# Three modulation vectors of an adaLN block: weights moving instead of stationary, with a transpose behind

## The chip, the cores and the metric

The kernel runs on one core of a Trainium2 chip. The metric is the device time of one execution in microseconds (us). Engines are named as the profile names them: PE is TensorE (PEld its weight loads), DVE is VectorE, ACT is ScalarE, POOL is GpSimd, and SP is the queue that issues most DMAs.

## The reference, cut to what matters

Two sub-blocks, a Mamba-like state-space layer and a stream-mixing layer, each stand behind a layer norm whose result is scaled and shifted by vectors made from a small conditioning input `c` (4 x 1024). A third vector gates each sub-block's output.

```python
mod = (_silu(L0_c) @ L0_wmod).reshape(4, 6, 1, -1)      # wmod is 1024 x 6144
sa, ca, ga, sb, cb, gb = (mod[:, i] for i in range(6))
ga = (2 * (ga >= 0) - 1) * jnp.maximum(jnp.abs(ga), 0.25)
gb = ...                                                # the same
h = _layernorm(x) * (1 + ca) + sa                       # x is 4 x 512 x 1024
x = x + ga * mamba(h, ...)                              # in_proj, conv, scan over time, out_proj
h = _layernorm(x) * (1 + cb) + sb
x = x + gb * mix_streams(h, ...)
```

All of it is fp32. This case is about `sa`, `ca` and `ga`.

## The kernel before

The work is split into 8 blocks (`NBLK`) of 256 time steps (`TB`), two to a batch row. A block of the scan has 64 steps: 4 groups of 512 channels by 16 state elements. One scan step has a product on POOL (`w`, L917), exponentials on ACT (`da`, L933), four scans on DVE (L963), eight transposes on PE (`hq`, L943) and two weighted sums on DVE (`acc`, L952).

Around the steps lie the matrix products: `pp` (L439) and `pz` (L487) are the in-projection, `po` (L667) the out-projection, `pd` (L597) the time-step projection. They are written as Python generators in one queue. Before the scan, the queue is run to its end (`whole()`), and the tile framework's scheduler sets the order of the instructions. In the scan the order is written out by hand: each step has six ticks, each tick lets the queue emit as many matmul columns as a rate allows (`paced`), and work that other code put on PE meanwhile is announced in columns with `aside` and taken off that rate. What follows a product, `finish()`, is spawned as a task that waits some ticks (`LAG` and others) before it emits. `take` and `give` count PSUM banks (`mm`, four) and SBUF rows (`row`, five); a waiting task tries again on a later tick.

Every product's weights come in tiles of 1 MB through three buffers (tag `wts`), loaded by SP (L218). `wmod` is cut in 24 such tiles: six kinds (`SA, CA, GA, SB, CB, GB`) by four quarters of 256 output columns.

There are two ways in which a kind is computed:

- `SA`, `CA` and `GA` (`product_mod`, L262): the weights are stationary, 128 x 128 at a time, and the 4 columns of `silu(c)` (`sc`) move through. The result comes out as 128 channels by 4 batch rows, all quarters in one PSUM bank, and one ACT instruction (L275 or L277) writes it to `mod_t`.
- `SB`, `CB` and `GB` (`product_rows`, L296): the 4 columns of `sc` are stationary and 256 columns of weights move. The result is 4 rows of 256, copied by ACT (L304) and stored to DRAM.

`SA` and `CA` are the first products of the kernel. `norm(0)` has loaded and normalized two tiles of `x` by then; it transposes them (L400) and scales and shifts them with `mod_t` (L409) into `ht`, on which `pp` of block 0 waits. After `whole()` the constants are loaded (`load_constants`). `GA` stands at the head of the queue in the scan of block 0, and `SB`, `CB`, `GB` come later in that block. `GA` is used first in block 1 (`product_out`).

Of the kernel before, what the change touches and what calls it, by code (L numbers as in the profile page):

```python
# [9 lines left out]
F32 = mybir.dt.float32  # L10
AF = mybir.ActivationFunctionType
# [5 lines left out]
P = 128  # L17
B, T, H = 4, 512, 1024
DIN, N, R, KC = 2048, 16, 64, 4
TB = 256  # L20
# [3 lines left out]
HC = H // P  # L24
# [8 lines left out]
LAG, TAP_LAG, ACT_LAG, POOL_LAG, DMA_LAG = 2, 3, 5, 10, 12  # L33
MAKE_UP = 1.3
TURN = 64
# [16 lines left out]
def adaln_block(  # L52
# [22 lines left out]
    vec, act, pool, pe = nc.vector, nc.scalar, nc.gpsimd, nc.tensor  # L75
# [7 lines left out]
    ident = const.tile([P, P], F32, name="ident")  # L83
# [17 lines left out]
    with ExitStack() as ph:  # L101
        p1 = ph.enter_context(tc.tile_pool(name="p1", bufs=1))
# [12 lines left out]
        done = set()  # L115
# [4 lines left out]
        def route(g):  # L120
            got = next(g, None)
            if got == "v":
                gaps.append(g)
            elif got is not None:
                waiting.append((clock[0] + max(got, 1), g))

        def spawn(g):
            route(g)

        def take(what, idle=1):  # L130
            while not free[what]:
                yield idle
            free[what] -= 1

        def give(what):
            free[what] += 1

        def until(key, idle=1):
            while key not in done:
                yield idle  # L140
# [58 lines left out]
        def aside(columns):  # L199

            owed[0] += columns
# [31 lines left out]
        def bank(name, shape):  # L233
            return ps_mm.tile(list(shape), F32, name=name, tag="mm")
# [4 lines left out]
        sc = p1.tile([P, HC, B], F32, name="sc")  # L239
# [5 lines left out]
        def away_from_zero(m, sg, ab):  # L245
            vec.tensor_scalar(sg, m, 0.0, 2.0, ALU.is_ge, ALU.mult)
            vec.tensor_scalar(ab, m, -1.0, 0.25, ALU.mult, ALU.max)
            vec.tensor_tensor(ab, ab, m, ALU.max)
            vec.scalar_tensor_tensor(m, sg, -1.0, ab, ALU.add, ALU.mult)

        pms = {}

        def product_mod(kind, q):

            if q == 0:
                yield from take("mm", 0)
                pms[kind] = bank(f"pm_{kind}", (P, HC, B))
            pm = pms[kind]
            w = weights.pop(("mod", kind, q))
            for j in range(2):  # L260
                for k in range(HC):
                    pe.matmul(  # L262
                        pm[:, 2 * q + j, :],
                        w[:, k, j * P : (j + 1) * P],
                        sc[:, k, :],
                        start=(k == 0),
                        stop=(k == HC - 1),
                    )
                    yield 128
            m = mod_t[:, kind]  # L270

            def finish():
                yield LAG
                if kind == CA:
                    act.activation(m, pm, AF.Copy, bias=1.0)  # L275
                else:
                    act.copy(m, pm)  # L277
                give("mm")
                if kind == GA:
                    yield ACT_LAG  # L280
                    yield "v"
                    sg = p1.tile([P, HC, B], F32, name="sg_ga", tag="ss")
                    ab = p1.tile([P, HC, B], F32, name="ab_ga", tag="sq")
                    away_from_zero(m, sg, ab)
                done.add(("mod", kind))

            if q == 3:
                spawn(finish())

        def product_rows(kind, q):  # L290

# [711 lines left out]
        with tc.manual_schedule():  # L1003
# [5 lines left out]
            for k in range(NBLK):  # L1009
# [9 lines left out]
                for s in range(STEPS):  # L1019
                    g = k * STEPS + s  # L1020
                    q, n = divmod(s, N)
# [15 lines left out]
    with ExitStack() as ph:  # L1037
        p1 = ph.enter_context(tc.tile_pool(name="f1", bufs=1))
# [29 lines left out]
        for i in range(NTT):  # L1068
            k, r = divmod(i, TT)
# [218 lines left out]
```

## Time and profile before

| what | value |
|---|---|
| three timed runs | 2709.05, 2709.85, 2709.86 us; median 2709.85 |
| the profiled execution | 2702.3 us, span 2700.5 us, mean granted TensorE clock 0.94 |
| L262, 128 x 4 | 384 records: 256 for SA and CA, 128 for GA |
| SA and CA on PE | first record at 9.06 us, `mod_t` complete at 66.50 us |
| first `pp` (L439) | 67.60 us |
| first scan step's transposes | 166.6 us |
| last GA record | 206.9 us |
| L296, 4 x 256 | 192 records, 271.4 to 331.4 us |

The profiled execution is one run, and its span is counted from the first to the last instruction. A row of the timeline gives start, duration, engine, line, operation, output and inputs with the count of merged instructions, and in brackets the idle time ahead of it and what ended that. A row of the windows gives, for a stretch of time, the busy time of each engine with its number of instructions, the granted clock, the busy share of the DMA engines and their GB/s. A busy TensorE is not one at its peak: the time of one record in a row of equal ones is better read from their spacing.

### The profile page before, as it was taken

What the parts mean: (1) busy time and instruction counts of PE and PEld (TensorE: products, weight loads), DVE (VectorE), ACT (ScalarE), POOL (GpSimd) and SP (SyncE); (2) the same over time, 40 slices, a digit from 0 to 9 for tenths busy, and PEclk for the clock granted to TensorE, in tenths of its full rate; (3) what the DMA queues carried; (4) which work ended last, traced back from release to release, by engine and by line L of the source; (5) the groups of instructions that cost most, each with busy time, mean ns of one, the idle gap of its engine ahead of it and who ended that gap; (6) DMA issues with size and microseconds to landing.
All of it is one profiled execution on the core that took longest, in us unless ns stands there. A gap on an engine that the chain in (4) does not pass through costs nothing. (4 is left out here: it accounts for less than half of the span.)

```text
span 2700.5 us, 39703 instructions
## 1 busy us (share of the span) xinstructions
PE 2408.1 (89%) x13392; PEld 2051.6 (76%) x13392; DVE 2361.0 (87%) x4451; ACT 1716.9 (64%) x3755; POOL 1731.8 (64%) x1167
## 2 busy tenths in 40 slices
PE   8999989999999989998999899998999899885446
PEld 8887478888788878887888788887888777675435
DVE  0349898999999999999999999999999899977898
ACT  0356567666776777667776776668666856633445
POOL 0146557777976688768766786779676977931014
PEclk9979989999999999999999999999999899896769
DMA  5432523333433343234333433333333323225302
GB/s 184 152 125 94 204 75 130 113 106 121 154 117 104 116 153 121 106 114 149 125 110 114 156 118 109 118 145 125 121 106 124 130 94 117 83 74 203 153 31 110
DMA packets 74347, 331.06 MB, mean 123 GB/s; under 512 B 8496, under 2 KB 25312, under 8 KB 47456
## 3 DMA queue, kind: packets, MB, share of 16 engines
q1 hardware_dynamic: 62784, 311.56, 32.1%
q10 hardware_dynamic: 11360, 16.96, 1.7%
q8 instruction: 107, 1.75, 0.3%
q14 instruction: 96, 0.79, 0.1%
HBM read 303.14 MB, written 25.35 MB: 122 GB/s over the span
## 5 line engine op out<-in xcount | busy, mean ns | idle before, releaser
L917 POOL TENSOR_TENSOR w<-u,b 128x1024 f32<-128x1024 f32 x512 | 1209.1, 2363 | 558.2 <-PE hq L943 413.5
L933 ACT ACTIVATE da<-dv,aneg 128x256 f32<-128x256 f32 x2048 | 971.5, 477 | 616.5 <-DVE w L963 571.5
L963 DVE TENSOR_TENSOR_SCAN w<-da,w 128x256 f32<-128x256 f32 x2048 | 1263.3, 667 | 69.5 <-ACT da L933 47.6
L952 DVE SCALAR_TENSOR_TENSOR acc<-hq,ss,acc 128x512 f32<-128x512 f32 x1024 | 724.6, 735 | 78.2 <-PE hq L943 73.1
L943 PE MATMUL hq<-ident,w 128*128 128x128 f32 x4096 | 644.1, 282 | 73.1 <-DVE acc L952 53.7
L943 PEld LDWEIGHTS hq<-ident,w 128*128 128x128 f32 x4096 | 511.8, 146 | 220.7 <-issue 57.7
L487 PE MATMUL pz<-w_z,ht 128*128 128x256 f32 x2048 | 517.2, 387 | 0.0
L439 PE MATMUL pp<-ht,w_x 128*128 128x259 f32 x2048 | 511.5, 387 | 0.0
L667 PE MATMUL po<-y,w_out 128*128 128x256 f32 x2048 | 496.2, 381 | 5.4 <-ACT dv L608 5.4
L439 PEld LDWEIGHTS pp<-ht,w_x 128*128 128x128 f32 x2048 | 372.1, 193 | 46.2 <-issue 0.4
L667 PEld LDWEIGHTS po<-y,w_out 128*128 128x128 f32 x2048 | 368.6, 191 | 46.5 <-ACT dv L608 6.9
L487 PEld LDWEIGHTS pz<-w_z,ht 128*128 128x128 f32 x2048 | 369.2, 195 | 36.5 <-issue 0.3
L455 DVE SCALAR_TENSOR_TENSOR xc<-pp,cw,xc 128x256 f32<-128x256 f32 x384 | 178.4, 464 | 31.8 <-ACT xc L448 30.7
L1212 POOL TENSOR_TENSOR o<-o,x 128x1024 f32<-128x1024 f32 x16 | 37.7, 2354 | 189.1 <-ACT dg L1158 142.2
L1197 PE MATMUL oa<-h,dg 128*128 128x256 f32 x256 | 62.8, 389 | 74.9 <-ACT dg L1158 69.5
L1197 PEld LDWEIGHTS oa<-h,dg 128*128 128x128 f32 x256 | 49.3, 195 | 84.1 <-ACT dg L1158 76.5
L467 POOL TENSOR_TENSOR xc<-xc,sx 128x1024 f32<-128x1024 f32 x32 | 75.5, 2358 | 42.8 <-ACT sx L465 42.8
L448 ACT ACTIVATE xc<-pp,cb,cw 128x256 f32<-128x256 f32 x128 | 71.3, 557 | 47.5 <-PE pp L439 47.4
L749 PE MATMUL py<-ident,acc 128*128 128x128 f32 x256 | 48.4, 324 | 54.7 <-ACT dv L608 28.3
L262 PEld LDWEIGHTS pm<-sc,w_mod 128*128 128x128 f32 x384 | 80.9, 323 | 9.0 <-DVE mv_a L358 9.0
L262 PE MATMUL pm<-sc,w_mod 128*128 128x4 f32 x384 | 79.5, 343 | 9.1 <-DMA w_mod<-wmod_dram 9.1
L749 PEld LDWEIGHTS py<-ident,acc 128*128 128x128 f32 x256 | 34.8, 167 | 67.2 <-ACT dv L608 25.2
(172 smaller groups left out, 2303.2 us busy)
## 6 DMA issues: line engine op xcount, KB each, us to landing
w_x<-in_w_dram SPq DMA_DIRECT2D x64, 1024.0 KB, 4.7
w_z<-in_w_dram SPq DMA_DIRECT2D x64, 1024.0 KB, 4.9
w_out<-out_w_dram SPq DMA_DIRECT2D x56, 1024.0 KB, 4.8
w_mod<-wmod_dram SPq DMA_DIRECT2D x24, 1024.0 KB, 4.8
b<-bcd SPq DMA_DIRECT2D x32, 512.0 KB, 3.8
xt<-x_dram SPq DMA_DIRECT2D x16, 512.0 KB, 8.2
xr<-x_dram SPq DMA_DIRECT2D x32, 256.0 KB, 5.1
x<-xr ACTq DMA_DIRECT2D x32, 256.0 KB, 2.5
```

The lines of the kernel that those rows point to most:

```text
L262: pe.matmul(pm[:, 2 * q + j, :], w[:, k, j * P : (j + 1) * P], sc[:, k, :], start=(k == 0), stop=(k == HC - 1),)
L439: pe.matmul(pp, w[:, h, j * P : (j + 1) * P], hts[k][:, h, :], start=(h == 0), stop=(h == HC - 1),)
L455: vec.scalar_tensor_tensor(xc[:, c, :], pp[:, tap : tap + TB], cw[:, i, tap : tap + 1], xc[:, c, :], ALU.mult, ALU.add,)
L487: pe.matmul(pz[:, t, :], hts[k][:, h, PAD + t * P : PAD + (t + 1) * P], w[:, h, :], start=(h == 0), stop=(h == HC - 1),)
L667: pe.matmul(po, w[:, d - lo, :], ys[k, d // QC][:, d % QC, :], start=(d == lo), stop=(d == hi - 1),)
L749: pe.transpose(py[:, j, t * P : (t + 1) * P], acc[:, t, c * P : (c + 1) * P], ident)
L917: pool.tensor_tensor(w, us[k, q], bts[k, n // NG][:, n % NG, :].unsqueeze(1).to_broadcast([P, QC, TB]), ALU.mult,)
L933: act.activation(da[:, j, :], dts[k, q][:, 2 * s + j, :], AF.Exp, scale=aneg[:, i, n : n + 1])
L943: pe.transpose(h[:, c * P : (c + 1) * P], ws[g][:, c, t * P : (t + 1) * P], ident)
L952: vec.scalar_tensor_tensor(acc[:, t, :], hqs.pop((g, t)), cts[k][:, t, n : n + 1], acc[:, t, :], ALU.mult, ALU.add,)
L963: vec.tensor_tensor_scan(w[:, c, :], das[g, c // 2][:, c % 2, :], w[:, c, :], 0.0, ALU.mult, ALU.add)
L1197: pe.matmul(oa[:, n, :], dg[:, n, m, :], hs[m] if m < NS else ybs[i], start=(m == 0), stop=(m == NS),)
```

## The change

`product_mod` now computes each quarter as `product_rows` does: `sc` is stationary, 256 weight columns move, and the result is 4 rows by 256 in a PSUM bank of its own. ACT copies each quarter into a row tile `mr` (4 x 1024). When the fourth quarter is there, eight transposes on PE bring the row into 128 channels by 4 batch rows (`pmt`), and ACT writes that to `mod_t` as before. The eight transposes are announced with `aside`. Nothing else is edited. Lines behind the edit move by 8: L439 becomes L447, L943 becomes L951.

```diff
-        pms = {}
+        mrows = {}
 
         def product_mod(kind, q):
 
-            if q == 0:
-                yield from take("mm", 0)
-                pms[kind] = bank(f"pm_{kind}", (P, HC, B))
-            pm = pms[kind]
+            yield from take("mm", 0)
             w = weights.pop(("mod", kind, q))
-            for j in range(2):
-                for k in range(HC):
-                    pe.matmul(
-                        pm[:, 2 * q + j, :],
-                        w[:, k, j * P : (j + 1) * P],
-                        sc[:, k, :],
-                        start=(k == 0),
-                        stop=(k == HC - 1),
-                    )
-                    yield 128
+            pm = bank(f"pm_{kind}_{q}", (B, TB))
+            for k in range(HC):
+                pe.matmul(pm, sc[:, k, :], w[:, k, :], start=(k == 0), stop=(k == HC - 1))
+                yield TB
             m = mod_t[:, kind]
 
             def finish():
                 yield LAG
+                if q == 0:
+                    yield from take("row")
+                    mrows[kind] = p1.tile([B, H], F32, name=f"mr_{kind}", tag="row", bufs=5)
+                    done.add(("mrow", kind))
+                yield from until(("mrow", kind))
+                mr = mrows[kind]
+                act.copy(mr[:, q * TB : (q + 1) * TB], pm)
+                give("mm")
+                if q < 3:
+                    return
+                yield LAG
+                yield from take("mm")
+                pt = bank(f"pmt_{kind}", (P, HC, B))
+                for i in range(HC):
+                    pe.transpose(pt[:, i, :], mr[:, i * P : (i + 1) * P], ident[:B, :B])
+                aside(HC * TURN // 2)
+                give("row")
+                yield LAG
                 if kind == CA:
-                    act.activation(m, pm, AF.Copy, bias=1.0)
+                    act.activation(m, pt, AF.Copy, bias=1.0)
                 else:
-                    act.copy(m, pm)
+                    act.copy(m, pt)
                 give("mm")
...
-            if q == 3:
-                spawn(finish())
+            spawn(finish())
```

## The prediction

> **What bounds the kernel now.** I read the page's busy shares first, then windows by stage, then TensorE's timeline where a stage is not like the others. Matmuls in fp32 leave two records each, transposes one; counts below are records.
>
> ```profile
> span 2700.5 us, 39703 instructions
> PE 2408.1 (89%) x13392; PEld 2051.6 (76%) x13392; DVE 2361.0 (87%) x4451; ACT 1716.9 (64%) x3755; POOL 1731.8 (64%) x1167
> ```
>
> The average names no bound: PE and DVE are level. By stage they part (columns: span, busy time and count of PE, PEld, DVE, ACT, POOL, granted TensorE clock, DMA share, GB/s):
>
> ```profile
> 9.03:43.00 33.97, 33.94 (x160) 33.97 (x161) 0.00 (x0) 2.56 (x3) 0.64 (x3) 1.00 0.46 172
> 184.06:191.53 7.47, 7.47 (x38) 7.47 (x37) 3.84 (x6) 3.55 (x9) 2.35 (x1) 0.50 0.36 132
> 280.00:324.52 44.52, 44.52 (x224) 18.97 (x223) 38.60 (x60) 21.13 (x56) 23.52 (x10) 1.00 0.59 206
> 860.00:1145.00 285.00, 270.26 (x1554) 233.15 (x1553) 268.14 (x462) 203.00 (x442) 215.06 (x143) 0.98 0.35 125
> ```
>
> The last line is the steady scan, where DVE has 17 us idle in 285. The first two are the stages of the edited product: PE has no idle time, DVE 0 or half. The third is the product of rows (L296), whose form the change copies. TensorE's timeline (start, duration, engine, line, operation):
>
> ```profile
> 9.06 34.26 PE L262 MATMUL pm<-sc,w_mod 128*128 128x4 f32 x160 [9.06 <-DMA w_mod<-wmod_dram]
> 43.19 2.80 PE L400 MATMUL pt<-ident,xt 128*128 128x128 f32 x12
> 45.78 20.48 PE L262 MATMUL pm<-sc,w_mod 128*128 128x4 f32 x96
> 66.55 1.11 PE L400 MATMUL pt<-ident,xt 128*128 128x128 f32 x4 [0.29 <-ACT mod_t L275]
> 67.60 58.94 PE L439 MATMUL pp<-ht,w_x 128*128 128x259 f32 x256
> ```
> ```profile
> 164.75 2.04 PE L400 MATMUL pt<-ident,xt 128*128 128x128 f32 x16
> 169.69 3.15 PE L262 MATMUL pm<-sc,w_mod 128*128 128x4 f32 x24
> 184.06 5.12 PE L262 MATMUL pm<-sc,w_mod 128*128 128x4 f32 x24
> 280.00 2.75 PE L296 MATMUL pmr<-w_mod,sc 128*4 128x256 f32 x12
> ```
>
> One L262 record costs 34.26/160 = 0.214 us at the start, 5.12/24 = 0.213 where the granted clock is 0.50, and 3.15/24 = 0.131 just before that. So the opening runs at half clock too, although its window prints 1.00 (transposes agree: 2.80/12 = 0.233 there, 2.04/16 = 0.128 at 164.75). One L296 record at full clock costs 0.2155 (2.75 us less the last one's 0.379, over 11).
>
> In the GA stage the waits of 166 to 208 say who is late:
>
> ```profile
> DVE acc L952 <- PE hq L943: 24.1, 11, 7.9
> ```
>
> DVE sits 24.1 us behind transposes that queue behind L262.
>
> **The change, part by part.** SA and CA at the start: 256 records go, 128 come.
>
> 1. Products. Removed: 256 x 0.214 = 54.7 us, all on the path. Added: 128 x 0.2155 = 27.6 us at full clock. Gain 27.1.
> 2. Clock. The first records still run at half. After L439 begins at 207.07 the granted clock is 0.83 from 208 to 212 and 1.00 after, so it came free some 2.5 us in; after the dt matmuls at 145.04 it took about 6 us. At half speed that loses 1.2 to 3 us. Taken: 2.5.
>
> Here a rule of the Trainium skill needs weighing (TensorE: Matmul & The Clock Gate, Part 1: The HAM clock gate): the clock is released after about 3.4 us of sustained matmuls. By the rule alone the opening would have been released by 13 us; the trace shows 57 us of unbroken L262 at the half-clock price, so being busy was not enough there. Whether the new product is enough is therefore read from L296: with the same 4-column weights and 256 moving columns the clock stays 1.00 for 44 us. The transposes around it do not explain that, as they are as many per step in the GA stage, at 0.50. By the rule or by L296 the sum is the 2.5 us above; by the L262 row (never released) 128 records cost 55 us and step 1 gains nothing. I take L296.
>
> 3. Tail, new on the path. As built, PE runs 8 transposes for SA, 6 for CA, three of the 16 x transposes, the last two for CA, then the other 13. A 4x128 to 128x4 transpose has no row; bounds are nothing and the half-clock L943 record (1.09/4 = 0.27); nearest is L262's own 128x4 record, so 0.131. From the last product to mod_t: 16 x 0.131 + 3 x 0.128 = 2.5 us on PE, which covers the last row copy (0.37 us by L304), then about 0.5 for the move into mod_t, then two L409 activations (1.07) before L439 begins: 4.1 us. Before, the same way was 66.26 (45.78 + 20.48) to 67.60, 1.3 us, and 12 x transposes (2.8) lay inside the products. Net: +2.8 for the longer tail, -2.8 for the transposes no longer there: 0.
>
> So L439 begins near 9.06 + 27.6 + 2.5 + 4.1 = 43.3, not 67.60: 24.3 us.
>
> 4. L439 itself. It starts at half clock now: 58.94 us against 128 x 2 x 0.2155 x 259/256 = 55.8 plus a last end, about 2.9 lost. A rule speaks against keeping this (same page, Part 4: PE-mode transpose: transposes do not count as busy for the clock); by it the 4 us tail of transposes cools the clock and the 2.9 stay lost. The row: 16 transposes at 164.75 and 8 after them run at 0.13 and the clock falls only at 172, over 5 us after the last wide product. I take the row, 2.9; the rule's zero goes into the range.
>
> 5. Loads. Hidden today by slow products, now closer. Each w_mod load is 1 MB and lands 4.8 us after issue; at 4 to 12 us the queue moves over 420 GB/s, 2.5 us per MB. A quarter now lasts 16 x 0.2155 = 3.45 us; its buffer's successor is wanted two quarters later, 6.9, against 4.8: 2.1 us slack. As built, five of the seven constant loads (0.6 MB, 0.4 to 0.6 us of SP each) stand between the w_mod loads instead of behind; dtw's half MB takes 1.3 of the slack. Zero taken; if the cover is gone, 2 to 4 us. The activation of aneg now stands before CA's last row copy on ACT; its load is issued after the last w_mod, three quarters (10 us) ahead: no wait. The row tiles of SA and CA make the second xt of block 1 wait on the first block's x transposes; on SP the ffn constants and the fourth w_x stand behind it, needed over 20 us later: zero.
>
> GA, in the scan. Removed: 128 records; added 64, 4 row copies, 8 transposes. DVE's scan groups begin at 172.24, 179.64, 184.97, 192.44, 200.33, 207.69, 213.10, then follow every 3.9 us or so. Up to 174.66 DVE is busy and nothing changes. The third group no longer waits behind slow dt matmuls and L262: about 177.6. The fourth then waits for ACT's two table loads and dv (until 180.06) and its da: 181.4. From there the mix is that of 280.00 to 324.52, ten steps in 44.52, 4.45 a step, PE-bound: 185.9, 190.3, 194.8, 199.2 against 213.10, 13.9 us. Eight transposes (1 us) and wide products landing in a step as before: 13. Bounds: 18 if steps fall to 4 us, 8 if the clock dips at the dt stage as it does at 332 to 342. The copies (368 ns by L304) lie on an ACT with half its time free; PSUM banks are now taken per quarter, as L296 does without starving PE.
>
> Later blocks. The three new notes of 256 aside columns hold the products back by 768/308 = 2.5 ticks, 0.4 of a step; as built the whole queue stands that much later in blocks 1 to 6, a b load goes ahead of a row load and that ahead of a w_z load on SP. DVE is the bound there and its instructions are the same. From 17 us idle per block I allow 2 either way in six blocks, 12, and take 0.
>
> Sum: 24.3 + 2.9 + 13 = 40 us. The profiled execution took 2702.3 (span 2700.5), so 2662; the three timed runs stand 7.5 us above it, and I expect that gap again: 2709.85 - 40 = 2670.
>
> **Rivals.** *Clock stays at half.* If four weight columns do not count as activity, and L296's clock was due to its company, a record costs twice 0.2155 = 0.43: 192 x 0.43 = 82.7 against 384 x 0.214 = 82.1, and 24 transposes at 0.27, late copies and the L439 start add 8: 2718, slower. It decides once the clock is at half for over three quarters of both stages. Against it: L296 at 1.00. For it: L262, busy and never released. 5%. *Start cold, GA full* (other products warm it there): the start loses about 5, GA keeps 13: 2702. 5%. *Loads bind*: if every load took the 8.8 us of the first (L218's longest), three buffers would turn over in 8.8 + 3.45, 4.1 us a quarter for 3.45, 3 us over five quarters; with 4 for the constants, 2677; inside the range, 10%. *Drift of the later blocks eats it*: 2 to 4 us in each of six blocks: 2682 to 2694; 8%, half inside. *The change misses the path*: not possible at the start, since nothing else runs there.
>
> **How the numbers follow.** The forecast 68%, loads 10%, drift 8% (half of it inside), a cold start 5%, a cold clock throughout 5%, better than 2656 by a drift the other way 4%. The range holds the first two and half of the third, 82%: 2656 is start 29, GA 18, drift +7; 2692 is start 20, GA 8, drift -10. Over 0.2% faster (5.4 us, about what a measurement of this kernel can tell): forecast, loads, better, most of drift and some of the cold start, 0.91; within 0.2%: the rest of those two, 0.04; slower: 0.05.
>
> **What would show it.** L259 records spaced 0.2155 from about 13 us on and 0.43 before; L439 beginning at 42 to 46; no w_mod wait on PE after the first; scan steps of 4.4 us in place of 7.4, hq waits of DVE before 200 us down from 24 to under 8; blocks of 285 us unchanged. Wrong: spacing near 0.43 past 20 us, holes on PE before a w_mod landing, or blocks of 288 and more.

## The result, and the profile after

The changed kernel takes 2703.43 us (median; 2699.0 to 2708.07) against 2709.98 us (2704.88 to 2717.91) for the kernel before, twelve runs each: the ratio is 0.9973, 95% interval 0.9964 to 0.9983. It is 6.5 us faster where 40 were forecast, and it lies outside the range of 2656 to 2692.

The first part of the working came out. TensorE's timeline of the changed kernel (start, duration, engine, line):

```profile
9.23 29.38 PE L259 MATMUL pm<-w_mod,sc 128*4 128x256 f32 x128 [9.23 <-DMA w_mod<-wmod_dram]
38.53 1.02 PE L279 MATMUL pmt<-ident,mr 4*128 4x4 f32 x14
39.49 0.55 PE L408 MATMUL pt<-ident,xt 128*128 128x128 f32 x3
39.97 0.28 PE L279 MATMUL pmt<-ident,mr 4*128 4x4 f32 x2
40.18 1.64 PE L408 MATMUL pt<-ident,xt 128*128 128x128 f32 x13
41.68 56.37 PE L447 MATMUL pp<-ht,w_x 128*128 128x259 f32 x256
```

All of SA and CA is one row of 128 records with a single wait ahead of it, the first load. `pp` begins at 41.68 us, was 67.60, and takes 56.37 us, was 58.94.

The steps of GA, in the same view later on:

```profile
151.66 2.75 PE L259 MATMUL pm<-w_mod,sc 128*4 128x256 f32 x12
156.04 2.75 PE L259 MATMUL pm<-w_mod,sc 128*4 128x256 f32 x12
169.70 0.65 PE L279 MATMUL pmt<-ident,mr 4*128 4x4 f32 x8
```

From 151.66 to 156.04 is one step of 4.4 us, the scan groups from 149.35 to 170.48 are 4.2 us apart on average, and GA is over at 170.35 (169.70 + 0.65). DVE's wait for transposes between 126 and 215 us, in the view of waits (total, times, longest), is 9.3 us, where 24.1 stood before (166 to 208 us); under 8 was forecast:

```profile
DVE acc L960 <- PE hq L951: 9.3, 4, 8.3
```

The longest wait in each sum does not belong to GA. It ends before the first GA record, which stands at 168.6 us before the change and at 142.6 after. DVE's timeline, before and after:

```profile
167.27 1.41 DVE L952 SCALAR_TENSOR_TENSOR acc<-hq,ss,acc 128x512 f32<-128x512 f32 x2 [7.85 <-PE hq L943]
140.54 1.41 DVE L960 SCALAR_TENSOR_TENSOR acc<-hq,ss,acc 128x512 f32<-128x512 f32 x2 [8.31 <-PE hq L951]
```

Without it, DVE waited 16.2 us in the GA stage before and 1.0 after.

So far the gain is there. Comparing when the same scan group begins in the two traces shows where it went (the first scan of each group of four on DVE, L963 before and L971 after):

| scan group | before, us | after, us | after less before (unrounded times) |
|---|---|---|---|
| block 0, step 0 | 154.6 | 127.4 | -27.2 |
| block 0, step 12 | 227.5 | 184.4 | -43.2 |
| block 1, step 0 | 470.4 | 432.1 | -38.3 |
| block 2, step 0 | 747.6 | 717.1 | -30.6 |
| block 3, step 0 | 1026.4 | 1004.1 | -22.3 |
| block 4, step 0 | 1306.9 | 1290.5 | -16.4 |
| block 5, step 0 | 1586.1 | 1577.5 | -8.6 |
| block 6, step 0 | 1867.3 | 1864.0 | -3.3 |
| block 7, step 0 | 2143.4 | 2148.4 | +5.1 |

The changed kernel was 43 us ahead at step 12 of block 0. Then each of blocks 1 to 6 took 5 to 8 us longer than before, and in the two profiled executions, of 2702.3 and 2703.51 us, all of the gain was given back; by the medians 6.5 us of it are left. The averages hardly tell: the page's busy shares, and the window of the prediction's steady scan (span, then busy time and count of PE, PEld, DVE, ACT, POOL, granted clock, DMA share, GB/s):

```profile
span 2701.6 us, 39388 instructions
PE 2384.0 (88%) x13224; PEld 1997.2 (74%) x13224; DVE 2362.9 (87%) x4451; ACT 1722.6 (64%) x3767; POOL 1732.1 (64%) x1167
```
```profile
860.00:1145.00 285.00, 265.46 (x1513) 229.17 (x1512) 261.58 (x451) 197.22 (x424) 212.29 (x147) 0.96 0.34 120
```

DVE, the bound of this stage, was busy 268.14 us in this window before and is now 261.58: 6.6 us of new idle time in about one block. The waits between 430 and 2150 us say what it waits for. Before:

```profile
DVE acc L952 <- PE hq L943: 23.7, 28, 2.0
PE hq L943 <- DVE acc L952: 18.3, 26, 2.6
PEld px L520 <- POOL xc L467: 2.2, 6, 0.5
PE px L520 <- POOL xc L467: 0.9, 3, 0.3
```

After:

```profile
DVE acc L960 <- PE hq L951: 63.2, 58, 2.9
PE hq L951 <- DVE acc L960: 52.7, 39, 4.7
POOL sz L512 <- ACT sgz L510: 26.0, 6, 4.7
PEld px L528 <- POOL xc L475: 17.4, 6, 3.2
PE px L528 <- POOL xc L475: 16.4, 6, 3.0
```

Each of the last three rows counts 6 waits in six blocks, one a block; in each an engine stands for another engine's result. POOL's wait for `sgz` has no row before the change. These rows are the leads that the experiments follow.

### The profile page after: what moved, and what is told of

It is laid out like the page before. It is cut to its first block, busy times and chain, and to the rows that moved or that the text cites. A ratio compares the mean times of both kernels' runs of the same rounds, so it can differ in the third digit from the quotient of the medians.

```text
span 2701.6 us, 39388 instructions
## 1 busy us (share of the span) xinstructions
PE 2384.0 (88%) x13224; PEld 1997.2 (74%) x13224; DVE 2362.9 (87%) x4451; ACT 1722.6 (64%) x3767; POOL 1732.1 (64%) x1167
## 5 line engine op out<-in xcount | busy, mean ns | idle before, releaser
L971 DVE TENSOR_TENSOR_SCAN w<-da,w 128x256 f32<-128x256 f32 x2048 | 1270.5, 669 | 88.5 <-ACT da L941 52.1
L951 PE MATMUL hq<-ident,w 128*128 128x128 f32 x4096 | 649.5, 285 | 97.4 <-DVE acc L960 87.6
L951 PEld LDWEIGHTS hq<-ident,w 128*128 128x128 f32 x4096 | 515.3, 147 | 257.5 <-issue 101.8
L447 PE MATMUL pp<-ht,w_x 128*128 128x259 f32 x2048 | 505.1, 384 | 1.3 <-issue 1.3
L675 PE MATMUL po<-y,w_out 128*128 128x256 f32 x2048 | 503.7, 384 | 0.0
L447 PEld LDWEIGHTS pp<-ht,w_x 128*128 128x128 f32 x2048 | 369.4, 191 | 46.4 <-issue 1.9
L1220 POOL TENSOR_TENSOR o<-o,x 128x1024 f32<-128x1024 f32 x16 | 37.7, 2353 | 189.6 <-ACT dg L1166 142.6
L512 POOL TENSOR_TENSOR sz<-sz,sgz 128x512 f32<-128x512 f32 x64 | 81.7, 1277 | 32.7 <-ACT sgz L510 32.7
L528 PE MATMUL px<-w_bc,xc 128*128 128x96 f32 x512 | 77.2, 311 | 20.9 <-POOL xc L475 20.9
L528 PEld LDWEIGHTS px<-w_bc,xc 128*128 128x128 f32 x512 | 74.5, 228 | 22.1 <-POOL xc L475 22.0
```

The costliest lines, as they stand in the source:

```text
L447: pe.matmul(pp, w[:, h, j * P : (j + 1) * P], hts[k][:, h, :], start=(h == 0), stop=(h == HC - 1),)
L512: pool.tensor_tensor(sz[:, :, s, :], sz[:, :, s, :], sg, ALU.mult)
L528: pe.matmul(px[:, t, :], xcs[k, i // QC][:, i % QC, t * P : (t + 1) * P], xpw[:, i, :], start=(i == 0), stop=(i == DC - 1),)
L675: pe.matmul(po, w[:, d - lo, :], ys[k, d // QC][:, d % QC, :], start=(d == lo), stop=(d == hi - 1),)
L951: pe.transpose(h[:, c * P : (c + 1) * P], ws[g][:, c, t * P : (t + 1) * P], ident)
L971: vec.tensor_tensor_scan(w[:, c, :], das[g, c // 2][:, c % 2, :], w[:, c, :], 0.0, ALU.mult, ALU.add)
```

## The experiments

Three theories stood at first. Q: the loss comes from the queue's position alone, which the change's three `aside` notes (768 columns) move back by 0.4 of a step. E: an earlier start is given back whatever the order. N: the new copies and transposes disturb the scan. When Q had been shown, the question was whether being late costs all along the block, or at a few places (theory S).

### The change without its aside

```diff
                     pe.transpose(pt[:, i, :], mr[:, i * P : (i + 1) * P], ident[:B, :B])
-                aside(HC * TURN // 2)
                 give("row")
```

> The change without its aside line, so that the product queue is told of no new columns. Theory Q (the three announcements of 256 columns put the whole product queue 0.4 of a step later in blocks 1 to 6, and that costs what the start and GA gain): the scan is 27 us ahead at its first step, 41 to 43 ahead at step 10, and stays 40 or so ahead in every block; 2669 us, against 2710 for the kernel before. Rival E (an earlier start is given back in the later blocks whatever their order): ahead by 41 at step 10, and level at block 7; 2703 as with the whole change. Rival N (the new row copies and transposes disturb the scan): the same 2703.

Measured: 2671.6 us (2661.54 to 2673.17), ratio to before 0.9857 (0.9839 to 0.9876). The scan groups stay ahead of the kernel before: -40.1 at the start of block 1, -37.1 at block 4, -35.8 at block 7. One line that costs no instruction is worth 32 us, and E and N fall with it: the start is as early and the copies and transposes are all there.

### The kernel before, with the same aside

```diff
             clock[0] = 0
+            aside(768)
```

> The kernel before, with 768 aside columns announced ahead of the first scan step and nothing else: no product is changed. Theory Q: start and GA as before, then 6 to 8 us lost in each of blocks 1 to 6, the same steps as in the changed kernel (44 to 60 above all); 2710 + 40 = 2750 us. Rivals E and N: 2710, no change.

Measured: 2748.94 us (2744.11 to 2749.47), ratio 1.0147 (1.0132 to 1.0162). Its scan groups fall behind those of before by +8.7 at block 1, +14.6, +22.9, +28.8, +36.5, +41.8 and +50.2 at block 7. The loss needs nothing of the new product: 768 columns of bookkeeping by themselves cost 40 us. It also loses them where the changed kernel does (the table of stretches below).

### SA and CA alone, GA alone, both without aside

```diff
-                    g = product_mod if kind in (SA, CA, GA) else product_rows
+                    g = product_mod if kind in (SA, CA) else product_mod_old if kind in (SA, CA, GA) else product_rows
```

`product_mod_old` is the product of the kernel before, put back beside the new one, and the `aside` line is left out (neither is shown here). The second kernel has `(GA,)` in place of the first `(SA, CA)`, so SA and CA take the old product.

> Only SA and CA in the new way, GA with stationary weights as before, no aside. Theory Q: the gain of the start alone, 27 to 28 us kept to the end: 2683 us. Rival E: given back, 2705 to 2710.

> Only GA in the new way, SA and CA as before, no aside. Theory Q: the gain of the GA stage alone, 13 to 15 us kept to the end: 2696 us. Rival E: given back, 2705 to 2710.

Measured: 2682.78 us, ratio 0.9907 (0.989 to 0.9923), for SA and CA; 2696.51 us, ratio 0.9959 (0.9944 to 0.9974), for GA. That is 25 and 11 us, together 36, against 39 for both at once: the two parts add up within 3 us, and both sizes of the prediction (24.3 + 2.9 = 27, and 13) hold to about 2 us.

### One place: the product xc on POOL

The tables below sum, over blocks 1 to 6, how much longer a stretch of steps took than in the change without its aside. In the changed kernel they come to 39.0 us over whole blocks: 20.2 us lie in steps 44 to 50 and 16.0 in steps 50 to 61. In the first stretch the loss begins with a hand-over at step 45, shown here in block 4. TensorE, POOL and DVE in the timeline of the changed kernel:

```profile
1485.31 2.82 PE L528 MATMUL px<-w_bc,xc 128*128 128x96 f32 x24
1491.17 2.02 PE L528 MATMUL px<-w_bc,xc 128*128 128x96 f32 x8 [3.04 <-POOL xc L475]
1492.98 1.06 PE L951 MATMUL hq<-ident,w 128*128 128x128 f32 x4
```
```profile
1486.46 2.35 POOL L925 TENSOR_TENSOR w<-u,b 128x1024 f32<-128x1024 f32 x1 [2.28 <-ACT state L988]
1488.77 2.34 POOL L475 TENSOR_TENSOR xc<-xc,sx 128x1024 f32<-128x1024 f32 x1
```
```profile
1488.79 2.42 DVE L971 TENSOR_TENSOR_SCAN w<-da,w 128x256 f32<-128x256 f32 x4
1494.08 0.75 DVE L960 SCALAR_TENSOR_TENSOR acc<-hq,ss,acc 128x512 f32<-128x512 f32 x1 [2.87 <-PE hq L951]
1497.85 2.42 DVE L971 TENSOR_TENSOR_SCAN w<-da,w 128x256 f32<-128x256 f32 x4
```

`px` (the B and C projection) needs `xc`, which POOL multiplies at 1488.77, behind the `w` of 1486.46. TensorE takes instructions in order, so it stands from 1488.13 to 1491.17, the transposes `hq` behind it start at 1492.98, and DVE's sum waits 2.87 us for them. From one scan group to the next 9.1 us pass. The same place without the aside, TensorE, POOL and DVE:

```profile
1464.71 2.26 PE L527 MATMUL px<-w_bc,xc 128*128 128x96 f32 x16
1466.81 0.60 PE L723 MATMUL pr<-ident,ao 128*128 128x128 f32 x4
1467.25 1.03 PE L527 MATMUL px<-w_bc,xc 128*128 128x96 f32 x8
1468.11 0.60 PE L950 MATMUL hq<-ident,w 128*128 128x128 f32 x4
```
```profile
1463.43 2.36 POOL L474 TENSOR_TENSOR xc<-xc,sx 128x1024 f32<-128x1024 f32 x1
1465.74 2.36 POOL L924 TENSOR_TENSOR w<-u,b 128x1024 f32<-128x1024 f32 x1
```
```profile
1466.85 1.25 DVE L970 TENSOR_TENSOR_SCAN w<-da,w 128x256 f32<-128x256 f32 x2
1471.09 1.83 DVE L970 TENSOR_TENSOR_SCAN w<-da,w 128x256 f32<-128x256 f32 x3
```

Here `xc` stands one place earlier in POOL's queue, ahead of the `w` and not behind it, `px` waits for nothing, and the groups are 4.2 us apart. Why a shift of 2.5 ticks moves `xc` by a whole step is read from the code: its task emits at a tick, and that tick now falls behind the one at which the step's `w` is emitted. The edit for this place alone, with the aside kept:

```diff
-                        yield ACT_LAG
+                        yield 3 if q == NQ - 1 else ACT_LAG
                         pool.tensor_tensor(xc, xc, sg, ALU.mult)
```

> The changed kernel whole, its aside included, with one task of the conv placed a slot earlier: POOL's product xc (L475) waits 3 ticks instead of ACT_LAG in the last quarter of a tile, so that it stands in POOL's queue at step 44 of a block, as in the kernel before, and not at step 45. Theory S (the loss of a block is that px waits on POOL's xc at step 46; this step alone is 3.6 us longer per block than in the kernel without the aside, of which about 1.3 comes back in the next two steps): six blocks give back 2 to 3.5 us each, 10 to 20 us in all, 2703 - 17 = 2686. Rival D (the loss is spread over everything that the queue emits later, and what is taken off at step 46 comes up elsewhere): 2700 to 2705.

Measured: 2680.52 us (2678.09 to 2683.23), ratio 0.989 (0.9873 to 0.9907): 23 us less than the changed kernel, more than the 10 to 20 expected. Steps 44 to 50 fell from +20.2 to -4.1, and steps 50 to 61 stayed at +16.0. The row of `px` waiting for `xc` is gone from the waits; the other once-a-block row, POOL's `sz` waiting for `sgz`, stays as it was (26.0 us, 6 times, 4.7 at the longest).

### A second place: the gate sz

That row belongs to steps 50 to 61. On ACT the softplus `dv` of the next block is bound to a step, with a table load ahead and one behind it, 1.28 + 1.57 + 1.28 = 4.1 us; the gate `sgz` of a z product rides on the queue. With the queue late, `dv` came first. In the timeline of c1_lag3, ACT and then POOL, POOL stands for 4.73 us before its gate, and `w` follows only then:

```profile
1506.80 1.28 ACT L616 ACT_TABLE_LOAD   x1
1508.09 1.57 ACT L616 ACTIVATE dv<-pd,dtb 128x256 f32<-128x256 f32 x4
1509.68 1.28 ACT L941 ACT_TABLE_LOAD   x1
1512.84 0.64 ACT L510 ACTIVATE sgz<-sgz 128x512 f32<-128x512 f32 x1
```
```profile
1513.56 1.26 POOL L512 TENSOR_TENSOR sz<-sz,sgz 128x512 f32<-128x512 f32 x1 [4.73 <-ACT sgz L510]
1514.78 2.36 POOL L925 TENSOR_TENSOR w<-u,b 128x1024 f32<-128x1024 f32 x1
```

The edit, on top of the last one, lets `dv` wait 5 ticks more, so that `sgz` stands ahead of it again, and takes the 5 ticks off the wait behind it. The instructions of TensorE, DVE and POOL keep their order. (A further line of the edit, not shown, sets a wait of the gate's task to 2 ticks, which `LAG` is already.)

```diff
-            yield LAG
+            yield 7 if k and q == 0 else LAG
             dv = quad_tile(f"dv_{k}_{q}", "dv", 2)
...
-            yield POOL_LAG
+            yield POOL_LAG - 5 if k and q == 0 else POOL_LAG
```

> The kernel c1_lag3 with one more pair put in its old order: on ACT, the gate sgz of the third z product stands ahead of the softplus dv of the next block (dv of a block's first quarter waits 7 ticks instead of LAG, and what follows it 5 ticks less). With the aside, dv and its two table loads (4.1 us on ACT) had come ahead of sgz, and POOL's sz (L512), with w behind it, waited 4.73 us a block for it. Theory S (two crossings make nearly the whole loss): steps 50 to 61, which cost 16.0 us in six blocks in c1_lag3 against the change without its aside, give most of that back: 2680.5 - 12 = 2668 (2664 to 2672), level with 2671.6 although the queue stands 0.4 of a step later. Rival R (dv later is itself as dear, or the loss at these steps is something else): 2678 to 2684.

Measured: 2670.01 us (2663.35 to 2672.38), ratio 0.9854 (0.9829 to 0.9878), as without the aside, though the queue is as late as in the changed kernel. The wait for `sgz` fell from 26.0 to 0.9 us:

```profile
POOL sz L512 <- ACT sgz L510: 0.9, 2, 0.4
```

Steps 50 to 61 fell from +16.0 to +6.1, not to zero: POOL's next `w` waits there now, 4.03 us for ACT, which still has to run `dv`. In the timeline, and in the waits between 430 and 2150 us:

```profile
1500.58 1.26 POOL L512 TENSOR_TENSOR sz<-sz,sgz 128x512 f32<-128x512 f32 x1 [0.44 <-ACT sgz L510]
1505.88 2.35 POOL L925 TENSOR_TENSOR w<-u,b 128x1024 f32<-128x1024 f32 x1 [4.03 <-ACT state L988]
```
```profile
POOL w L925 <- ACT state L988: 12.0, 3, 4.0
```

The three waits are in blocks 2, 4 and 6, and so is the whole rest (+7.7 us; blocks 1, 3 and 5 have -1.6). By the code only the first block of a batch row has this `state` copy on ACT. No run moved it.

### The first place alone, in a queue that is not late

```diff
-                        yield ACT_LAG
+                        yield 7 if q == NQ - 1 else ACT_LAG
                         pool.tensor_tensor(xc, xc, sg, ALU.mult)
```

> The change without its aside (2671.6), with POOL's product xc of the last quarter made to wait 7 ticks instead of ACT_LAG: it then stands in POOL's queue at step 45 of a block, as in the changed kernel, while the queue keeps the position of the kernel before. Theory S (this place by itself makes 24 us of the loss): 2671.6 + 24 = 2696 (2688 to 2700), all at step 45 of blocks 1 to 6. Rival P (the place hurts only together with the late queue): 2670 to 2678.

Measured: 2690.96 us (2688.77 to 2691.81), ratio 0.9933 (0.9917 to 0.9949), 20 us above the same kernel without this edit. Nearly all of it lies at that place (+18.3 in steps 44 to 50, 0.0 in 50 to 61), and the row is back:

```profile
PE px L527 <- POOL xc L474: 11.2, 6, 2.0
```

So this crossing costs about 20 us whether the queue is late or not. The kernels side by side:

| longer than the change without aside, us in blocks 1 to 6 | steps 44 to 50 | steps 50 to 61 | median, us |
|---|---|---|---|
| the change | +20.2 | +16.0 | 2703.43 |
| the kernel before | -1.1 | +0.6 | 2709.98 |
| the kernel before with 768 columns of aside (b1_before_late) | +20.2 | +16.0 | 2748.94 |
| xc mended (c1_lag3) | -4.1 | +16.0 | 2680.52 |
| xc and sgz mended (c2_both) | -4.1 | +6.1 | 2670.01 |
| no aside, xc made late (d1_lag7) | +18.3 | 0.0 | 2690.96 |

The profiled run of the change without aside took 2661.54 us, the shortest of its four, so sums against its trace come out some microseconds larger than differences of medians (39 us against 32 over whole blocks for the change). Differences between the other rows are free of that: 20.2 less -4.1 is 24 us where the medians say 23.

### Other positions of the queue

The change without its aside, with a note of -384, -768 or +384 columns ahead of the first scan step.

```diff
             clock[0] = 0
+            aside(-384)
```

> The change without its aside, and 384 columns taken off the queue's debt ahead of the first scan step, so that the whole queue stands 0.2 of a step earlier in every block than in the kernel before. Theory Q in its linear form (1000 columns later cost about 53 us, by the 768 columns of the kernel before with an aside, which cost 40): 384 earlier are worth 20 us more than the 2671.6 of the change without aside, 2651. Rival S (the loss comes from a few places where an instruction crosses a slot of the order, and the position of the kernel before lies on the good side of them): 2668 to 2680.

> The same with 768 columns taken off, 0.4 of a step earlier. Theory Q in its linear form: 2631. Rival S (single places): no slope; 2665 to 2690, since other instructions then cross their slots.

> The change without its aside, and 384 columns added to the queue's debt ahead of the first scan step, half of what the change's own asides add. Theory Q in its linear form: 2671.6 + 20 = 2692. Rival S: either about 2672 (xc of POOL not yet moved to step 45) or near the whole loss, 2700 and more (moved), not halfway.

Measured, from early to late: 2673.8 us at -768 (ratio 0.9865, 0.9848 to 0.9882), 2660.9 at -384 (0.9814, 0.9797 to 0.9831), 2671.6 at 0, 2681.7 at +384 (0.9884, 0.9859 to 0.9908), with the change itself, at +768, at 2703.4. A line would have gone on down to 2631 at -768; the time turns back up there. Both theories missed something: -384 lies below the band given for S, and +384 is a third of the way to +768 (10 of 32 us), which S as put there excluded.

The traces show where the time goes. At -768 `xc` stands ahead of the `w`, as in the kernel before, but `px` waits for it again, at step 44 of each block: +17.4 us in that step, of which later steps give back a part (+6.7 over steps 44 to 50). At +384 `px` has no wait for `xc`, and the loss is at step 36 (+14.3): once a block the in-projection `pp` stands 3 us for `dv` on ACT, a wait that the change without its aside does not have. The rows of -768 and of +384 (430 to 2110 us):

```profile
PE px L527 <- POOL xc L474: 11.3, 6, 2.0
```
```profile
PE pp L446 <- ACT dv L615: 18.0, 6, 3.1
```

POOL's wait for `sgz` is back at +384 too, 14.1 us where the change has 26.0. So the positions show single places and no slope; that these places make the times at -768 and +384 is read from the traces and was not tested by an edit.

-384 is the fastest version that was run, and beats both kernels. Whose gain is it? The same line in the kernel before:

> The kernel before, with 384 columns taken off the queue's debt ahead of the first scan step and nothing of the change. If the 11 us by which the change without aside gained from the same 384 columns belong to the later blocks alone, the kernel before gains them too: 2710 - 11 = 2699 (2695 to 2703). Rival: they come with the change's GA in block 0, and the kernel before stays at 2706 to 2714.

Measured: 2695.03 us (2694.27 to 2700.79), ratio 0.9959 (0.9942 to 0.9975). Eleven of its microseconds belong to the queue's position and are to be had without the change (0.0041 of 2707); some 39 more are the change (0.9814 / 0.9959 = 0.9854).

## Why the prediction was wrong

The direction was right; the forecast missed by 33 us, nearly all in one step.

1. Products and clock (27.1 less 2.5): held. 29.38 us for 128 records against 27.6 at full clock is 1.8 lost at the start (7 records in the 2.77 us up to 12 us, 19 in the next 4.00), 2.5 taken. The L296 row was the right witness: 256 columns moving through 4-column weights brought the clock up, where L262 in the opening never had; with the L262 row the gain would have been nothing.
2. Tail (4.1 us): 38.53 to 41.68 is 3.15. The transposes came cheaper than the 0.131 taken: 14 in 1.02 us, 0.07 each.
3. The start of `pp`: 43.3 forecast, 41.68 measured, 25.9 us earlier, 24.3 forecast.
4. `pp` warm from its start (2.9): 58.94 to 56.37, 2.6. The row gave the right size, and not the zero that the prediction drew from the rule weighed beside it (the Trainium skill, TensorE: Matmul & The Clock Gate, Part 4: PE-mode transpose, by which transposes do not count as busy): a tail of 3.15 us, mostly transposes, did not bring `pp` back to its cold 58.94. What a longer row of them would do, no run here shows. `pp` ends 28.5 us earlier than before and the scan begins 27.2 earlier; that this equals 24.3 + 2.9 to the tenth is luck.
5. Loads at zero: held. No wait for `w_mod` after the first.
6. GA (13): from -27.2 at the first scan group to -43.2 at step 12, 16 us in the two traces; 11 by the run of GA alone. Within the bounds of 8 to 18. Two readings beside it were wrong without changing the sum: 7.9 of DVE's 24.1 us ended before the first L262 record of GA, and the six groups after 213.10 follow 4.4 to 4.8 us apart, not 3.9.
7. Later blocks: this is the step that failed. It saw the mechanism, 768 columns, 2.5 ticks, 0.4 of a step, and priced it as "I allow 2 either way in six blocks, 12, and take 0", from DVE's 17 us of idle time a block. Measured is 5 to 8 us a block in one direction, 40 us for the kernel before and 32 for the change by the medians. The error was to take a bound engine's average slack as cover. The order does not spread a delay over a block: at one tick `xc` changes sides with a `w`, and 4 us appear at one step (24 us in six blocks); `sgz` and `dv` change sides at another, for 10 us by the medians. Nor is the loss alike in size from one position to the next: with the queue at -768, -384, 0, +384 and +768 columns `px` waited 11.3, 3.7, 0.9, 0 and 16.4 us for `xc` in six blocks.

Among the rivals "drift of the later blocks" had the right place, at 2 to 4 us a block and 8%. With the 32 us that the aside cost by the medians, its own sum is 2709.85 - 40 + 32 = 2702. The other rivals, a cold clock, a cold start and binding loads, did not occur.

In the list of what would show it, "blocks of 288 and more" was put as the sign of a wrong forecast. Blocks of 284 to 287 us were enough, because the yardstick was wrong too: 285 was the length of a window, and blocks 1 to 6 of before take 276 to 281.

## What to carry to other kernels

In an order written out by hand, a note of cost that emits nothing is still an edit of every later instruction: compare the order of each engine before and after, and price each pair that changes sides by what waits behind it on its engine. The busy share of the bounding engine does not say where a shift will hurt. A small wait that occurs once in every block can: `px` waiting for `xc` was such a row here (PEld's, 6 times and 2.2 us before the change). But not every place shows beforehand, as `sgz` had no row. When a gain at the start does not reach the end, compare the starts of the same step in both traces: a loss that grows by the same amount in each block is a place in the loop, and its step number finds it.

## What the hardware did that was not expected

The stall for `xc` costs TensorE more than its 3.04 us. Windows of the changed kernel around it:

```profile
1485.00:1488.10 3.10, 3.10 (x28) 2.96 (x27) 2.74 (x5) 3.02 (x8) 1.64 (x1) 1.00 0.90 309
1491.10:1494.00 2.90, 2.83 (x14) 2.84 (x14) 0.11 (x1) 1.07 (x3) 0.01 (x1) 0.50 0.00 0
1494.00:1496.30 2.30, 2.30 (x13) 2.30 (x12) 0.75 (x1) 0.00 (x0) 0.47 (x1) 0.50 0.00 0
```

The granted clock is 1.00 before the stall and 0.50 for 5 us behind it. Eight `px` records take 2.02 us there, 1.03 in the kernel without the stall, and four `hq` 1.06 instead of 0.60, just when DVE waits for them. Without the stall the clock is 1.00 at the same place. The windows of the change without its aside, and of d1_lag7 behind its stall of 1.77 us for `xc`, where the clock fell as well:

```profile
1466.00:1471.00 5.00, 5.00 (x47) 5.00 (x48) 5.00 (x9) 2.76 (x8) 3.40 (x2) 1.00 0.23 85
1486.00:1488.00 2.00, 2.00 (x12) 2.00 (x11) 0.51 (x1) 0.47 (x2) 0.00 (x0) 0.50 0.39 131
```

So in the changed kernel 3 us of waiting became 4.8 us between two scan groups (9.1 against 4.2); how much each of stall and clock holds was not separated by a run.

The opening had less in reserve than the missing waits suggest: its window shows DMA engines busy to 0.89 at 316 GB/s.

```profile
9.23:41.68 32.45, 32.45 (x161) 14.17 (x161) 0.29 (x1) 7.04 (x16) 0.17 (x1) 1.00 0.89 316
```

What stays open: whether the three waits of `w` for `state` make the 6 us that steps 50 to 61 still cost with both places mended, and what makes -384 the best position. Its trace is 6.6 us shorter in steps 44 to 50 and 3.1 in steps 50 to 61 than that of the change without aside, although `px` waits longer for `xc` there.
